# Layer 1's expert-weight products: five float32 values a node, or nine bf16 pairs on 96 partitions

## The chip, the cores and the metric

The kernel runs on one core of a Trainium2 chip, as one program. The metric is the device time of one execution in microseconds (us). The core's engines each work through a list of their own, in order: PE (matrix products; its weight loads are shown as PEld), DVE (vectors), ACT (activation functions and copies), POOL (here mostly the issue of gathers by index) and SP (the issue of plain transfers). Where one needs what another makes, it waits on a semaphore.

## The reference

A graph of 6250 nodes with 256 features and 106250 edges goes through two layers. Layer 0 is a two-step graph convolution, a linear attention and a feed-forward block with eight experts, one for each node. Layer 1 is a graph mean, a channel attention with an MLP, and a feed-forward block with four experts, two for each node, beside a shared MLP. The change concerns that last block:

```python
xn = _layernorm(x)
x = x + _L1_gnn_ref(xn, ...) + _L1_mix_ref(xn[None], ...)[0]
f = _layernorm(x)
# _L1_ffn_ref(f):
h = relu(einsum('baf,efh->ebah', f, eW1) + eb1)       # 4 experts, 256 -> 128
h = relu(einsum('ebah,ehg->ebag', h, eW2) + eb2)      # 128 -> 64
all_out = einsum('ebag,ego->ebao', h, eW3) + eb3      # 64 -> 256
shared = (three layers: sW1, sW2, sW3, with biases)   # 256 -> 256 -> 128 -> 256
topv, topi = top_k(softmax(f @ gW + gb), 2)
topw = softmax(topv)
out = shared + sum over the two chosen experts of topw * all_out
x = x + out
```

So every node has four expert weights (two of them zero) and the constant 1 for the shared bias: five numbers, called `we` below. The output must be float32 and agree with the reference.

## The kernel before

Nodes are held in 49 tiles of 128 rows (`NT`), edges in 831 chunks of 128 (`NCH`), sorted by destination, about 17 chunks to a node tile (`PER`). There are three passes over the edges. In each, POOL gathers the 128 source rows of a chunk by index (L542, one instruction a chunk, issued four at a time into one of three buffers in layer 1), DVE makes one-hot matrices for four chunks (L546), and PE multiplies the rows with the one-hots into running sums (L565). The first pass gathers float32 rows; the second and third gather rows that were split beforehand into three bf16 parts which add up to the float32 number exactly, so that a chunk is six short bf16 products.

Before the first pass, the edges are sorted into place, the rows are normalized, and a first table `t1f` is written by SP (L317) from DVE's and ACT's rows. The second pass also holds layer 0's expert block: `route` finds each node's expert and its slot, counts the nodes of each expert (`count`, L944) and sends the rows to their slots a planned 16 us later (`send`, by `later`); `pick` reads `count` to choose the next expert whose 128 rows are served.

The third pass is layer 1. Two jobs run beside its sums, each on a group of two node tiles, 25 groups in all:

- `mixing` (L1379 on): normalize, transpose (`xn3tr`, L263), attention product `att` (L1397), statistics, transpose (`hmtr`, L1412), fc1 with Gelu on ACT (L1420, L1422), fc2 on top of the self product `ws` (L1428, L1432).
- `feed` (L1451 on): the neighbour product (`neigh`, L1462), statistics, transpose (`f3tr`), the gate (L1482) and its softmax and top-two selection in about two dozen small DVE operations that end with `we` (L1509); the shared MLP (`s1`, `s2`) and the experts' first layer (`e1`, L1524, evacuated by DVE at L1526); then the part of the change: `we` is transposed to five rows `wet` (L1537, copied by ACT at L1538); the second expert layer for a pair of experts (L1545); `wexp` (L1550) spreads the weights over the pair's 128 hidden rows by a product with the selection matrix `sel`; DVE multiplies (L1551); and the output sums the shared product (L1558), the biases weighted by `wet` (`eb3`, L1559, with the shared bias `sb3` as the fifth row) and the two pairs (L1561). DVE adds the input and SP stores.

The order on PE, SP and POOL is written out by a planner, `pace` (L593 on): every `yield a, b` of a job says that the part just issued takes `a` us and that its result is there `b` us later; a chunk of sums is given 1.25 us in all, of which 0.23 us are its own. Between two chunks the planner issues those parts of the jobs that are due. When a job has nothing due, only chunks are issued. A feed starts when the sums of its two tiles are issued and its mixing is done; mixing starts at most six tiles ahead of the sums. What is left when the chunks are over is issued at the end (`rest`). The order on DVE and ACT is chosen by the compiler's scheduler. ACT loads a table whenever it goes from one of Sqrt, Exp and Gelu to another.

PSUM in layer 1 has four banks for products, used in turn (`mm`), one for transposes (`tr`), one for accumulation (`acc`) and two for sums. The constants `eb3`, `sel`, `wets` are made at the start of layer 1 (L1235 to L1238, L1265 to L1268, L1273 to L1277), partly by POOL ahead of its first gather there.

Of the kernel before, what the change touches and what calls it, by code (L numbers as in the profile page):

```python
# [31 lines left out]
F32 = mybir.dt.float32  # L32
BF16 = mybir.dt.bfloat16
I32 = mybir.dt.int32
AF = mybir.ActivationFunctionType
ALU = mybir.AluOpType
AX = mybir.AxisListType

P = 128
N = 6250  # L40
C = 256
# [63 lines left out]
NEXP = 8  # L105
# [33 lines left out]
def gps_kernel(ctx: ExitStack, tc: tile.TileContext, i: dict, out: bass.AP):  # L139
# [68 lines left out]
    rank8 = consts.tile([P, 8], F32, name="rank8")  # L208
    nc.vector.tensor_scalar(rank8, iota_f[:, :8], -1.0, 8.0, op0=ALU.mult, op1=ALU.add)

    deg = consts.tile([P, NT], F32, name="deg")
    dinv = consts.tile([P, NT], F32, name="dinv")
    rdeg = consts.tile([P, NT], F32, name="rdeg")
# [442 lines left out]
    nc.sync.dma_start(wout, i["L0_mix_W_out"])  # L656
    nc.sync.dma_start(boutr, row_bcast(i["L0_mix_b_out"], C))

    general_sums(t1, True)


# [235 lines left out]
    def route(v, t0, n):  # L897

        w = n * P
        f = work.tile([P, 2, C + 1], F32, name="f", bufs=3)  # L900
        for t in range(n):
            T = t0 + t
            normalize(f[:, t, :C], xa[:, T, :], mv1[:, T, :], rs1[:, T:T + 1])
        nc.vector.tensor_copy(f[:, :n, C:], mark[:, t0:t0 + n, None])
        yield 0.0, 4.0
        ft = work.tile([P, 2, 2 * P], F32, name="ft")
        transposed(ft, lambda t: f[:, t, :], n, "ftr", vs)
        yield 0.45 * n, 1.0
        for ht in hidden(ft, w):
            yield 0.43 * n, 0.0  # L910
        lt = ps_acc("gate")[:NEXP, :w]
        for m in range(8):
            nc.tensor.matmul(lt, lhsT=wg[:, m, :], rhs=ht[:, m, :w], start=(m == 0), stop=(m == 7))
            if m % 2 and m < 7:
                yield 0.43 * n, 0.0
        ls = work.tile([NEXP, 2 * P], F32, name="ls")
        nc.vector.tensor_scalar(ls[:, :w], lt, bgc, None, op0=ALU.add)
        yield 0.43 * n, 1.0
        tr = ps_tr("gate_t")
        for t in range(n):  # L920
# [12 lines left out]
        nc.vector.tensor_copy(ob, one)  # L933
        yield 0.3 * n, 6.0

        before = ps_acc("rank")[:, :n * NEXP]
        for t in range(n):
            b = before[:, t * NEXP:(t + 1) * NEXP]
            nc.tensor.matmul(b, lhsT=onesb, rhs=run[v], start=True, stop=False)
            nc.tensor.matmul(b, lhsT=upto, rhs=ob[:, t, :], start=False, stop=True)  # L940
            nc.vector.tensor_add(run[v], run[v], ob[:, t, :])
        cp = ps_tr("count")[:1, :NEXP]
        nc.tensor.matmul(cp, lhsT=onesb[:, 0:1], rhs=run[v], start=True, stop=True)
        nc.vector.tensor_copy(count[v], cp)  # L944
        at = small.tile([P, n, NEXP], F32, name="at")
        nc.vector.tensor_tensor(at, before.rearrange("p (t e) -> p t e", e=NEXP),
                                rb[v][:, None, :].to_broadcast([P, n, NEXP]), op=ALU.add)
        nc.vector.tensor_mul(at, at, one)
        to = small.tile([P, n], F32, name="slotf")
        nc.vector.tensor_reduce(to, at, AX.X, ALU.add)  # L950
        nc.vector.tensor_copy(slots[:, t0:t0 + n], to)
        yield 0.2 * n, 0.0

        def send():
            for t in range(n):
                r = rows_of(t0 + t)
                nc.gpsimd.indirect_dma_start(
                    out=xs[v][:, :], out_offset=bass.IndirectOffsetOnAxis(ap=slots[:r, t0 + t:t0 + t + 1], axis=0),
                    in_=f[:r, t, :], in_offset=None)
            routed[0] = t0 + n  # L960

        later(lag[0], send)
# [267 lines left out]
    for e in range(4):  # L1230
# [1 line left out]
        nc.sync.dma_start(ew1[:, :, e, :], i["L1_ffn_eW1"][e].rearrange("(k p) h -> p k h", p=P))  # L1232
        nc.sync.dma_start(ew2[:, e, half * 64:half * 64 + 64], i["L1_ffn_eW2"][e])
        nc.sync.dma_start(ew3[half * 64:half * 64 + 64, e // 2, :], i["L1_ffn_eW3"][e])
    eb3 = wl.tile([P, C], F32, name="eb3")  # L1235
    nc.gpsimd.memset(eb3, 0.0)
    nc.sync.dma_start(eb3[0:4, :], i["L1_ffn_eb3"])
    nc.sync.dma_start(eb3[4:5, :], i["L1_ffn_sb3"][None, :])  # L1238
    bfc1 = wl.tile([P, 6], F32, name="bfc1")
    nc.sync.dma_start(bfc1, columns(i["L1_mix_b_fc1"], 6))  # L1240
    ng = wl.tile([P, 2], F32, name="ng")
# [18 lines left out]
    nc.gpsimd.tensor_add(bsum, bsum, bf2r)  # L1260
    bxf = wl.tile([P, C], F32, name="bxf")


    seli = wl.tile([5, 2, 2, 64], I32, name="seli")
    nc.gpsimd.iota(seli, pattern=[[2, 2], [1, 2], [0, 64]], base=0, channel_multiplier=-1)  # L1265
    sel = wl.tile([P, 2, P], F32, name="sel")
    nc.gpsimd.memset(sel, 0.0)
    nc.vector.tensor_scalar(sel[:5], seli.rearrange("p a b c -> p a (b c)"), 0.0, None, op0=ALU.is_equal)  # L1268
    wstack = ExitStack()
    work = pool(wstack, "work3", bufs=1)  # L1270


    wets = []  # L1273
    for b in range(2):
        wet = wl.tile([P, 2 * P], F32, name=f"wet{b}")
        nc.gpsimd.memset(wet, 0.0)
        wets.append(wet)  # L1277

    xos = []
    for b in range(3):  # L1280
# [170 lines left out]
    def feed(t0, n):  # L1451
# [55 lines left out]
        nc.vector.tensor_tensor(o2, o2, d[:, :, None].to_broadcast(bc), op=ALU.mult)  # L1507
        nc.vector.tensor_add(o1, o1, o2)
        nc.vector.tensor_tensor(we[:, :, 0:4], o1, rd[:, :, None].to_broadcast(bc), op=ALU.mult)  # L1509
        yield 0.5 * n, 0.0  # L1510

        s1t = work.tile([P, 2, 2 * P], F32, name="s1t")
# [21 lines left out]
        wet = wets[t0 // 2 % 2]  # L1534
        tr = ps_tr("wet")
        for t in range(n):
            nc.tensor.transpose(tr[:5, t * P:(t + 1) * P], we[:, t, :], ident)  # L1537
        nc.scalar.copy(wet[:5, :w], tr[:5, :w])  # L1538
        yield 0.2 * n, 0.8

        e2t = work.tile([P, 2, 2 * P], F32, name="e2t")
        for pair in range(2):
            e_ps = ps_mm("e2_ps")
            for e in range(2):
                nc.tensor.matmul(e_ps[:, :w], lhsT=ew2[:, 2 * pair + e, :], rhs=e1t[:, 2 * pair + e, :w],  # L1545
                                 start=(e == 0), stop=(e == 1))
            nc.scalar.activation(e2t[:, pair, :w], e_ps[:, :w], AF.Relu, bias=eb2[:, pair:pair + 1], scale=1.0)
            yield 0.43 * n, 0.0
            w_ps = ps_mm("wexp")
            nc.tensor.matmul(w_ps[:, :w], lhsT=sel[:, pair, :], rhs=wet[:, :w], start=True, stop=True)  # L1550
            nc.vector.tensor_mul(e2t[:, pair, :w], e2t[:, pair, :w], w_ps[:, :w])  # L1551
            yield 0.22 * n, 0.0
        yield 0.0, 0.8

        for t in range(n):
# [4 lines left out]
            for pair in range(2):  # L1560
                nc.tensor.matmul(y, lhsT=e2t[:, pair, s], rhs=ew3[:, pair, :], start=False, stop=(pair == 1))  # L1561
            nc.vector.tensor_add(x3[:, t, :], x3[:, t, :], y)
            yield 1.72, 0.0
        if t0 + n < NT:
            nc.sync.dma_start(tiles_of(out, t0, n), x3[:, :n, :])
        else:
# [40 lines left out]
```

## Time and profile before

| | |
|---|---|
| median of 13 runs | 4452.33 us (4441.56 to 4474.08) |
| the profiled execution's own time | 4448.36 us |
| its span, first to last instruction | 4446.4 us |
| busy: PE / PE weight loads / DVE / ACT / POOL | 3309.8 / 2719.3 / 1417.8 / 949.7 / 2543.6 us |
| before the first pass's sums | 0 to about 98 us |
| layer 1, from its first instruction on POOL to the end | 3070.9 to 4446.4 us |
| wexp in layer 1 (L1550): PE records, busy | 100, 33.0 us |
| biases by weights (L1559): PE records, busy | 98, 30.2 us |
| transposes of `we` (L1537): PE records, busy | 49, 9.6 us |
| table loads on ACT in layer 1 | 79, 1283 ns each |

All times are from one profiled execution. The busy time of PE is the sum of durations of pipelined matmuls, which overlap; the distance between two starts says how long a matmul holds PE. A float32 product is two PE records, a bf16 product one. In the groups of instructions, out and in are tile names without buffer numbers; in the list of waits stand the total, how often, and the longest. In the timeline a row merges equal instructions in a row: start, length, count, and the idle time before it.

### The profile page before, as it was taken

What the parts mean: (1) busy time and instruction counts of PE and PEld (TensorE: products, weight loads), DVE (VectorE), ACT (ScalarE), POOL (GpSimd) and SP (SyncE); (2) the same over time, 40 slices, a digit from 0 to 9 for tenths busy, and PEclk for the clock granted to TensorE, in tenths of its full rate; (3) what the DMA queues carried; (4) which work ended last, traced back from release to release, by engine and by line L of the source; (5) the groups of instructions that cost most, each with busy time, mean ns of one, the idle gap of its engine ahead of it and who ended that gap; (6) DMA issues with size and microseconds to landing.
All of it is one profiled execution on the core that took longest, in us unless ns stands there. A gap on an engine that the chain in (4) does not pass through costs nothing. (4 is left out here: it accounts for less than half of the span.)

```text
span 4446.4 us, 60555 instructions
## 1 busy us (share of the span) xinstructions
PE 3309.8 (74%) x23423; PEld 2719.3 (61%) x23423; DVE 1417.8 (32%) x5275; ACT 949.7 (21%) x2019; POOL 2543.6 (57%) x2665
## 2 busy tenths in 40 slices
PE   3788776667655657877777788884788888888888
PEld 2577666666553446655555566663576676676676
DVE  6222222122221222222223322644433333443333
ACT  3111000000001112232222223441122222222222
POOL 1666666666656666666666565112666666666562
PEclk9888766666666678888888898997899999999999
DMA  4466433433344455555555665575444444444442
GB/s 154 132 169 167 119 114 116 116 116 116 115 127 135 125 147 158 172 174 172 172 164 160 202 188 158 178 238 156 124 133 127 133 129 128 131 129 134 130 129 68
DMA packets 341389, 639.63 MB, mean 144 GB/s; under 512 B 57498, under 2 KB 230341, under 8 KB 341088
## 3 DMA queue, kind: packets, MB, share of 16 engines
q0 software_dynamic: 151872, 450.67, 35.3%
q1 hardware_dynamic: 188366, 184.56, 13.5%
q8 instruction: 185, 3.03, 0.3%
q14 instruction: 116, 0.95, 0.1%
q10 hardware_dynamic: 850, 0.43, 0.0%
HBM read 559.64 MB, written 75.80 MB: 143 GB/s over the span
## 5 line engine op out<-in xcount | busy, mean ns | idle before, releaser
L542 POOL DMA_INDIRECT parts<-t3b,sp x831 | 807.4, 972 | 506.6 <-issue 199.1
L542 POOL DMA_INDIRECT parts<-t2b,sp x831 | 806.9, 971 | 486.6 <-issue 221.0
L542 POOL DMA_INDIRECT rows<-t1f,sp x831 | 804.1, 968 | 482.8 <-issue 225.3
L565 PEld LDWEIGHTS <-parts 128*128 128x128 bf16 x9972 | 600.5, 107 | 349.0 <-issue 138.4
L565 PE MATMUL sums<-onehotf,rows 128*128 128x84 f32 (+1 forms) x3324 | 595.8, 328 | 291.7 <-issue 224.3
L565 PEld LDWEIGHTS sums<-onehotf,rows 128*128 128x128 f32 x3324 | 579.9, 247 | 342.3 <-issue 311.2
L565 PE MATMUL sums<-onehot,parts 128*128 128x84 bf16 (+2 forms) x9972 | 687.1, 215 | 107.3 <-DMA parts<-t2b,sp 54.2
L892 PE MATMUL hid<-ft,fw 128*128 128x256 f32 (+1 forms) x1824 | 549.4, 441 | 45.6 <-ACT ht L894 28.1
L546 DVE TENSOR_TENSOR onehot<-iota_w,lof 128x336 bf16<-128x336 bf16 x416 | 210.2, 506 | 744.1 <-PE sums L565 314.8
L892 PEld LDWEIGHTS hid<-ft,fw 128*128 128x128 f32 x1824 | 370.1, 221 | 106.0 <-ACT ht L894 32.9
L894 ACT ACTIVATE ht<-hid,fb 128x256 f32<-128x256 f32 (+1 forms) x456 | 209.7, 472 | 437.6 <-PE hid L892 263.1
L546 DVE TENSOR_TENSOR onehotf<-iota_wf,lof 128x336 f32<-128x336 f32 x208 | 104.0, 507 | 623.3 <-remote 454.3
L1075 PE MATMUL exp<-wd,ht 128*128 128x256 f32 x1024 | 259.5, 391 | 5.6 <-ACT ht L894 5.6
L768 PE MATMUL h<-w,aggt 128*128 128x256 f32 x392 | 156.1, 538 | 107.6 <-DVE aggt L586 48.4
L585 ACT COPY aggt<-sums 128x88 f32<-128x88 f32 x96 | 22.4, 233 | 865.6 <-PE sums L565 538.6
L1075 PEld LDWEIGHTS exp<-wd,ht 128*128 128x128 f32 x1024 | 185.8, 192 | 30.4 <-ACT ht L894 8.5
L1047 POOL DMA_INDIRECT ys<-y,to x64 | 63.6, 994 | 220.9 <-DVE y L1080 76.1
L768 PEld LDWEIGHTS h<-w,aggt 128*128 128x128 f32 x392 | 93.2, 263 | 129.7 <-DVE aggt L586 51.8
L1420 PE MATMUL fc_ps<-ht,fc 128*128 128x256 f32 (+1 forms) x600 | 162.5, 394 | 1.7 <-issue 1.1
L1432 PE MATMUL fc_ps<-fc,ut 128*128 128x256 f32 x588 | 159.3, 395 | 3.7 <-issue 3.5
L1420 PEld LDWEIGHTS fc_ps<-ht,fc 128*128 128x128 f32 x600 | 106.8, 196 | 12.1 <-issue 1.1
L1432 PEld LDWEIGHTS fc_ps<-fc,ut 128*128 128x128 f32 x588 | 103.2, 191 | 14.2 <-issue 5.0
(354 smaller groups left out, 4274.2 us busy)
## 6 DMA issues: line engine op xcount, KB each, us to landing
wd<-in_L_ffn_Wd SPq DMA_DIRECT2D x64, 1024.0 KB
xs<-zero SPq DMA_DIRECT2D x8, 1799.0 KB
rows<-t1f,sp POOLq DMA_INDIRECT x831
parts<-t2b,sp POOLq DMA_INDIRECT x831
parts<-t3b,sp POOLq DMA_INDIRECT x831
t2b<-t2s SPq DMA_DIRECT2D x49, 192.0 KB
t3b<-t3s SPq DMA_DIRECT2D x24, 384.0 KB
fs<-xs SPq DMA_DIRECT2D x64, 128.5 KB
```

Of the source, the lines that this page charges most:

```text
L542: nc.gpsimd.indirect_dma_start(out=gs[:, j, :], out_offset=None, in_=(table if f32 else parts)[:, :], in_offset=bass.IndirectOffsetOnAxis( ...
L546: nc.vector.tensor_tensor(ohs[:, :n, :], (iota_wf if f32 else iota_w)[:, None, :WIN].to_broadcast([P, n, WIN]), lof[:, c:c + n, None].to_b ...
L565: nc.tensor.matmul(ps[b][:, h, n0 - b * P:n1 - b * P], lhsT=g[:, k * C + h * P:k * C + (h + 1) * P], rhs=oh[:, n0 - w0:n1 - w0], start=Fal ...
L585: nc.scalar.copy(dst[:, :, WIN:], sums[:, :, WIN:P])
L768: nc.tensor.matmul(h, lhsT=at[:, k, :], rhs=w[:, k, :], start=(k == 0), stop=(k == 1))
L892: nc.tensor.matmul(h_ps[:, :w], lhsT=fw1[:, k, m * P:(m + 1) * P], rhs=ft[:, k, :w], start=(k == 0), stop=(k == 1))
L894: nc.scalar.activation(ht[:, m, :w], h_ps[:, :w], AF.Gelu, bias=fb1[:, m:m + 1], scale=1.0)
L1047: nc.gpsimd.indirect_dma_start(out=ys[v][:, :], out_offset=bass.IndirectOffsetOnAxis(ap=to, axis=0), in_=y, in_offset=None)
L1075: nc.tensor.matmul(y_ps, lhsT=ht[:, m, q * P:(q + 1) * P], rhs=wd[:, m, :], start=(m == 0), stop=(m == 7))
L1420: nc.tensor.matmul(u_ps[:, :w], lhsT=fc1[:, k, m * P:(m + 1) * P], rhs=ht[:, k, :w], start=(k == 0), stop=(k == 1))
L1432: nc.tensor.matmul(h_ps, lhsT=ut[:, m, t * P:(t + 1) * P], rhs=fc2[:, m, :], start=False, stop=(m == 5))
```

## The change

`we` is split into three bf16 parts on DVE that add up to it exactly (`wes`, six copies with repetition and two subtractions for a group of two tiles). The 15 columns of a row are five values of part 0, then of part 1, then of part 2, and this row stands three times, at columns 0, 32 and 64 (the rest stays zero). The transpose becomes a product with a bf16 identity, which gives 96 rows. `sel` holds ones for all parts in all three places; `eb3` holds the three exact bf16 parts of the biases, part j in rows 32j and on, each repeated for the three parts of the weights. So one bf16 product sums all nine pairs of parts, where a float32 product stood. The constants move to the start of the program, with nine loads of the expert biases and three of the shared bias in place of one each; POOL's five fills at the start of layer 1 go. The planned times of the parts are made smaller. Apart from that, layer 0's `count` is set when the rows are sent, by way of a small copy, and not when they are counted.

```diff
+    identb = consts.tile([P, P], BF16, name="identb")
+    nc.vector.tensor_copy(identb, ident)
+    sel = consts.tile([P, 2, P], BF16, name="sel")
+    eb3 = consts.tile([P, C], BF16, name="eb3")
+    wets = [consts.tile([P, 2 * P], BF16, name=f"wet{b}") for b in range(2)]
+    wes = [consts.tile([P, 2, 3, 32], BF16, name=f"we{b}") for b in range(2)]
+    for b in range(2):
+        nc.vector.memset(wets[b], 0.0)
+        nc.vector.memset(wes[b], 0.0)
...
+        seli = early.tile([P, 2, 2, 64], I32, name="seli")
+        nc.gpsimd.iota(seli, pattern=[[2, 2], [1, 2], [0, 64]], base=0, channel_multiplier=-1)
+        self_ = early.tile([P, 2 * P], F32, name="self")
+        nc.vector.tensor_copy(self_, seli.rearrange("p a b c -> p (a b c)"))
...
+        nc.vector.tensor_scalar(acc, self_, 0.0, None, op0=ALU.is_equal)
+        for k in (-5.0, -10.0):
+            nc.vector.tensor_scalar(one, self_, k, None, op0=ALU.is_equal)
+            nc.vector.tensor_add(acc, acc, one)
+        nc.vector.tensor_copy(sel.rearrange("p a m -> p (a m)"), acc)
+        whole3 = early.tile([P, C], F32, name="eb3w")
+        nc.vector.memset(whole3, 0.0)
+        for j in range(3):
+            for k in range(3):
+                nc.sync.dma_start(whole3[32 * j + 5 * k:32 * j + 5 * k + 4, :], i["L1_ffn_eb3"])
+            nc.sync.dma_start(whole3[32 * j + 4:32 * j + 5, :], i["L1_ffn_sb3"][None, :])
+        part = early.tile([P, C], BF16, name="eb3p")
+        for j in range(3):
+            s = slice(32 * j, 32 * j + 32)
+            nc.vector.tensor_copy(part, whole3)
+            nc.vector.tensor_copy(eb3[s, :], part[s, :])
+            nc.vector.tensor_sub(whole3, whole3, part)
+        nc.vector.memset(eb3[96:, :], 0.0)
...
-        nc.vector.tensor_copy(count[v], cp)
+        soon = small.tile([1, NEXP], F32, name="counted", bufs=4)
+        nc.vector.tensor_copy(soon, cp)
...
+            nc.vector.tensor_copy(count[v], soon)
             routed[0] = t0 + n
...
-    eb3 = wl.tile([P, C], F32, name="eb3")
-    nc.gpsimd.memset(eb3, 0.0)
-    nc.sync.dma_start(eb3[0:4, :], i["L1_ffn_eb3"])
-    nc.sync.dma_start(eb3[4:5, :], i["L1_ffn_sb3"][None, :])
...
-    seli = wl.tile([5, 2, 2, 64], I32, name="seli")
-    nc.gpsimd.iota(seli, pattern=[[2, 2], [1, 2], [0, 64]], base=0, channel_multiplier=-1)
-    sel = wl.tile([P, 2, P], F32, name="sel")
-    nc.gpsimd.memset(sel, 0.0)
-    nc.vector.tensor_scalar(sel[:5], seli.rearrange("p a b c -> p a (b c)"), 0.0, None, op0=ALU.is_equal)
...
-        wet = wl.tile([P, 2 * P], F32, name=f"wet{b}")
-        nc.gpsimd.memset(wet, 0.0)
...
+        wb = wes[t0 // 2 % 2]
+        for k in range(3):
+            at3 = [wb[:, t, :, 5 * k:5 * k + 5] for t in range(n)]
+            for t in range(n):
+                nc.vector.tensor_copy(at3[t], we[:, t, None, :].to_broadcast([P, 3, 5]))
+            if k < 2:
+                nc.vector.tensor_sub(we, we, wb[:, :n, 0, 5 * k:5 * k + 5])
         yield 0.5 * n, 0.0
...
-            nc.tensor.transpose(tr[:5, t * P:(t + 1) * P], we[:, t, :], ident)
-        nc.scalar.copy(wet[:5, :w], tr[:5, :w])
-        yield 0.2 * n, 0.8
+            nc.tensor.matmul(tr[:96, t * P:(t + 1) * P], lhsT=wb[:, t].rearrange("p j r -> p (j r)"), rhs=identb,
+                             start=True, stop=True)
+        nc.scalar.copy(wet[:96, :w], tr[:96, :w])
+        yield 0.07 * n, 0.8
...
-            yield 0.22 * n, 0.0
+            yield 0.06 * n, 0.0
...
-            yield 1.72, 0.0
+            yield 1.4, 0.0
```

The lines of the two products themselves (L1550, L1559) stay as they are; their operands are now bf16. In the built program the lists of the first two passes keep their order on PE, and that of layer 1 on PE, DVE and ACT is another one.

More of the change, by code (lines that the diff above doesn't have):

```diff
@@ L657, in gps_kernel @@
     nc.sync.dma_start(boutr, row_bcast(i["L0_mix_b_out"], C))
+    with ExitStack() as st:
+        early = pool(st, "early")
+        seli = early.tile([P, 2, 2, 64], I32, name="seli")
+        nc.gpsimd.iota(seli, pattern=[[2, 2], [1, 2], [0, 64]], base=0, channel_multiplier=-1)
+        self_ = early.tile([P, 2 * P], F32, name="self")
+        nc.vector.tensor_copy(self_, seli.rearrange("p a b c -> p (a b c)"))
+        one = early.tile([P, 2 * P], F32, name="selone")
+        acc = early.tile([P, 2 * P], F32, name="selacc")
+        nc.vector.tensor_scalar(acc, self_, 0.0, None, op0=ALU.is_equal)
[16 more added lines that the diff above has]
+        nc.vector.memset(eb3[96:, :], 0.0)
     general_sums(t1, True)
@@ L1261, in gps_kernel @@
     bxf = wl.tile([P, C], F32, name="bxf")
-    seli = wl.tile([5, 2, 2, 64], I32, name="seli")
-    nc.gpsimd.iota(seli, pattern=[[2, 2], [1, 2], [0, 64]], base=0, channel_multiplier=-1)
-    sel = wl.tile([P, 2, P], F32, name="sel")
-    nc.gpsimd.memset(sel, 0.0)
-    nc.vector.tensor_scalar(sel[:5], seli.rearrange("p a b c -> p a (b c)"), 0.0, None, op0=ALU.is_equal)
     wstack = ExitStack()
     work = pool(wstack, "work3", bufs=1)
-    wets = []
-    for b in range(2):
-        wet = wl.tile([P, 2 * P], F32, name=f"wet{b}")
-        nc.gpsimd.memset(wet, 0.0)
-        wets.append(wet)
     xos = []
```

## The prediction

> **What bounds the kernel now.** I read the page's busy rows and slices first, then the busy time by stage.
>
> ```profile
> PE 3309.8 (74%) x23423; PEld 2719.3 (61%) x23423; DVE 1417.8 (32%) x5275; ACT 949.7 (21%) x2019; POOL 2543.6 (57%) x2665
> PE   3788776667655657877777788884788888888888
> POOL 1666666666656666666666565112666666666562
> 3200.00:4390.00 1190.00, 1012.71 (x7998) 828.18 (x7997) 472.07 (x1655) 272.32 (x574) 726.95 (x749) 0.93 0.46 130
> 4390.00:4446.40 56.40, 40.95 (x226) 34.76 (x223) 21.03 (x89) 16.94 (x35) 0.00 (x0) 0.90 0.03 11
> ```
>
> The columns of the last two lines are stretch, length, then busy time of PE, PEld, DVE, ACT, POOL, then clock. All edited products lie after 3200 us, in layer 1. There PE is busy 85% at a granted clock of 0.93, POOL 61%, DVE 40%, ACT 23%. Who is waited for there, in the list of waits of PE from 3070 us on (total us, times, longest):
>
> ```profile
> PE xn3tr L263 <- DVE xnt L267: 43.8, 18, 5.2
> PE f3tr L263 <- DVE ft L267: 38.3, 25, 5.5
> PE hmtr L1412 <- DVE ht L1413: 16.1, 18, 2.9
> PE sums L565 <- DMA parts<-t3b,sp: 11.9, 1, 11.9
> PE ffn L1558 <- DVE x L1562: 10.3, 9, 3.1
> PE wet L1537 <- DVE we L1509: 2.9, 1, 2.9
> ```
>
> The gathers starve PE once; the rest are chains through DVE and ACT before a transpose. L1486 (once a group) starts at 3214.9 and, 22 groups on, at 4355.5: 51.8 us a group, of some 34 chunks, while POOL could issue 34 gathers in 34 x 1.25 = 42.5 us (below). So PE's in-order stream sets the pace: its own work, plus waits in front of three transposes, none of them in the edited lines.
>
> **What one edited product costs.** Timelines of PE and POOL, and the chain of waits near the end:
>
> ```profile
> 3997.37 1.10 PE L1524 MATMUL e_ps<-ft,ew 128*128 128x256 f32 x4
> 3998.31 0.39 PE L565 MATMUL sums<-onehot,parts 128*128 128x84 bf16 x6
> 3998.53 1.10 PE L1524 MATMUL e_ps<-ft,ew 128*128 128x256 f32 x4
> 3581.78 0.34 PE L558 MATMUL sums<-zrow 128*128 128x424 bf16 x1
> 3581.96 0.39 PE L565 MATMUL sums<-onehot,parts 128*128 128x84 bf16 x6
> 4412.40 0.22 PE wet L1537 x2
> 4415.22 0.43 PE wexp L1550 x2
> 4419.10 0.43 PE ffn L1559 x2
> 3564.67 0.94 POOL L542 DMA_INDIRECT parts<-t3b,sp  x1 [0.30 <-issue]
> ```
>
> Durations overlap, so prices are distances between starts. A float32 product is two records: 0.43 us on the chain (0.94 for two in the timeline). A bf16 matmul of 424 columns holds PE 3581.96-3581.78 = 0.18 us, so 256 columns take 0.108; six of 84 columns, with six weight loads, take 0.22, which gives 0.112. The built program has each edited product as one load and one matmul.
>
> - wexp (L1550): 48 x (0.43-0.108) + 2 half-wide x 0.16 = 15.8 us off PE.
> - eb3 (L1559): 49 x 0.322 = 15.8 us off.
> - wet (L1537): 49 x (0.11-0.055) = 2.7 us off.
>
> Together **-34.3 us** of PE time, before anything replaces it. Bounds: -38 by the 0.94 row, 0 if every saving turns into waiting (rival 2).
>
> **What is added.**
>
> - *DVE splits* (six copies, two subtractions a group, 197 in all). Nearest row: L1509, 128x8, 168 ns; bounds 60 ns (memset L1506) and 411 ns (copy L267), so 12 to 81 us of DVE work, 33 at 168 ns, 1.35 us a group. They sit behind L1509 and ahead of two e1t evacuations (L1526), whose PSUM banks come round again four tiles later, and ahead of one-hots that are three buffers deep. In the group at 3580 us L1509 started at 3588.59 and wet at 3593.92: 5 us of cover. If it were gone, wet would wait. The last group has no cover: five operations, 0.85 us. I take **+2**, range 0 to +33.
> - *ACT order.* In the built program layer 1 has 79 table loads before and 100 after. From about the fifteenth group on, Gelu is cut by Exp twice and Sqrt once. Cause: the smaller yields (each feed is planned 1.5 us shorter) let feed catch up with the gathers, after which it waits for its next sums tile and drifts against mixing. Before, one group has that pattern, the last two-tile one:
>
> ```profile
> 4405.42 1.28 ACT L1422
> 4407.10 1.28 ACT L1501
> 4409.52 1.13 PE L1524 MATMUL e_ps<-ft,ew 128*128 128x256 f32 x4 [0.25 <-DVE e1t L1526]
> ```
>
> Both loads are on the chain, yet PE idled only 0.25 us after them, since other products were queued. So 21 x 1.283 = 27 us if all show, some 3 if all are covered like this. Behind a load wait Gelu, s1t and the d that DVE needs for wet; s1t's banks are needed four products on. Nearer the covered end, I take a quarter, **+7**.
>
> The Trainium skill (ScalarE: Activation LUTs, What ACT_TABLE_LOAD costs) speaks against this change: it gives 1283 ns for the load and some 1380 ns more for a drain. By that page 21 switches would be an estimated 56 us and the change a loss. This trace has the 1.28 but not the drain: the Gelu after the load at 4405.42 started at 4406.71.
>
> - *The drift itself.* After the drift the order puts three to five chunks of sums before the transposes hmtr and f3tr; four chunks are 4 x 0.22 = 0.9 us of PE, while att to hmtr needs 0.41+0.42+0.17+0.30+0.16+0.78 = 2.2 us through L1399, L223, L224, L228, L229, L232. But xn3tr no longer comes right behind neigh's statistics, and mixing's and feed's chains run side by side, so the 43.8 and 38.3 us of waits above may shrink. Unsigned: **0**, from -40 to +48 (rivals 1 and 3).
> - *Early block.* Twelve loads at 0.43 us on SP: six stand before the first t1f store (they wait for a memset behind DVE's work that ends at 70.5; the store went at 74.11), five in the gap up to 78.35, one after the last store. Eight DVE operations (0.31 to 0.42 each) fill DVE's idle 2.83 us before 73.32; the nine of the split wait for the loads but stand behind the first one-hots, with 8 us idle before 105.95. If that cover were gone: 12 x 0.43 = 5. **+0.5**, range 0 to +5. POOL's early iota lies far ahead of its first gather (98.4).
> - *Count repair.* 25 copies of 1x8 on DVE, 0.17 us at most each, in a stage where DVE is under a third busy; the same number of chunks is served, perhaps in another order of experts: **0**, range 0 to +4.
> - ACT's copy of wet goes from 5 to 96 partitions with the same 256 columns (354 ns): 0.
>
> **What is moved.** Five POOL fills leave the start of layer 1, where the chain of waits passes through POOL's first gather:
>
> ```profile
> 3071.33 0.31 POOL L1236 MEMSET eb<- 128x256 f32 x1
> 3072.87 1.00 POOL L542 DMA_INDIRECT parts<-t3b,sp  x1 [0.17 <-issue]
> ```
>
> **-1.5 us**; bounds 0 (if DVE's one-hot at 3073.37 holds PE) and -1.5. The two SP loads removed there are not waited for. The tail: after the last sums (4395.6) the old order still has a mixing and two feeds, the new one the end of a feed and one more. PE work is only shifted, but of the old tail's 45 us about 10 are waits (from 4390 on 56.4 less 41 busy, less the 5.8 after PE's end at 4440.6); I take **-3**, from 0 to -10. The chain through neigh, f3tr, gate and wet of the last tile stays.
>
> **Sum:** -34.3 +2 +7 +0 +0.5 +0 -1.5 -3 = -29. The profiled execution took 4448.36 us (span 4446.4), 4 under the median 4452.33; it would become 4419, and the median **4423**.
>
> **Rivals.**
>
> 1. *Slower:* in the last ten groups the table loads and the uncovered att chain land on PE. For it: both loads on the chain at 4405; against: PE idled 0.25 us there. Price: two loads and the 2.2 us chain are 4.8 us a group, 48 in ten; in place of the +7 this gives -36+48 = +12: 4464. It decides from 3.6 us a group.
> 2. *No change:* PE reaches the three transposes earlier and waits the difference. For it: those waits total 98 us and DVE sets their ends. Against: L1550 and L1559 stand eight or more products before them, and DVE is 60% idle. Price: 4450.
> 3. *Much faster:* the new phase removes waits, and groups approach POOL's 42.5 us. Ten groups, 4 us each of the 9 between: -40 more, 4383; all nine 4333.
>
> That the products are not cheaper is excluded by the bf16 rows.
>
> **Numbers.** 0.2% is 9 us, about what a measurement of this kernel can tell from no change. Forecast (4395 to 4443) 0.60; rival 1 0.14; rival 2 0.12; rival 3 0.14. Faster 0.60+0.14 = 0.74, same 0.12, slower 0.14. The range leaves out about a tenth on each side: 4380, inside rival 3, to 4462, inside rival 1.
>
> **What would show it.** Wexp and ffn L1559 at one record each, some 0.11 us apart; 50 and 49 rows for 100 and 98; PE busy after 3200 us down by some 35; the first gather of layer 1 1.5 us earlier after L1228; 100 table loads in layer 1, their cost seen as PE waits for ut (L1422 in the old numbering) and hmtr in the last 400 us. Wrong if the early groups, with their order nearly unchanged, do not shrink from 52 to about 50.5 us, or if the last ten grow past 54.

## The result, and the profile after

The change made the kernel slower where a gain of 29 us had been forecast: a median of 4484.34 us (4476.75 to 4509.75, 11 runs) against 4457.35 us for the kernel before (48 runs), ratio 1.0074 with a 95% interval of 1.0059 to 1.0090. The profiled execution of the changed kernel took 4458.62 us (span 4456.8), 26 us under its median, where that of the kernel before lay 9 us under its own; two profiles alone would have shown 10 us for a loss of 27 by the medians and 33 by the ratio.

Page rows of the changed kernel, and its busy time by stage (stretch, length, then PE, PEld, DVE, ACT, POOL, PE's granted clock, DMA share, GB/s):

```profile
PE 3301.7 (74%) x23324; PEld 2702.2 (61%) x23324; DVE 1459.7 (33%) x5519; ACT 976.7 (22%) x2040; POOL 2544.7 (57%) x2661
PE   3788766767655667787777878784788888888877
3200.00:4390.00 1190.00, 987.73 (x7764) 801.41 (x7763) 499.89 (x1832) 298.18 (x590) 710.09 (x732) 0.90 0.45 127
4390.00:4456.80 66.80, 46.08 (x353) 37.26 (x350) 25.14 (x107) 17.87 (x39) 16.82 (x18) 0.93 0.22 65
```

In the same 1190 us PE is busy 25 us less than before, and less is done (732 instructions on POOL, not 749). The granted clock is 0.90, not 0.93; the prediction had read that figure and then left it alone.

The three edited products and the table loads on ACT (two views of the changed kernel: instructions by line with duration min/median/max, then groups with total and mean):

```profile
L1585 PE MATMUL wexp<-wet,sel x50: 216/272/417, 3234.2 to 4448.0; 128*128 128x256 bf16 x48, 128*128 128x128 bf16 x2
L1594 PE MATMUL ffn<-eb,wet x49: 269/273/421, 3240.3 to 4449.1; 128*128 128x256 bf16 x49
L1541 DVE CAST we<-we 128x15 bf16<-128x15 f32 x147 | 19.7, 182 | 2.1
L1543 DVE TENSOR_TENSOR we<-we,we 128x10 f32<-128x10 f32 (+1 forms) x50 | 8.5, 170 | 1.3
L1448 ACT ACT_TABLE_LOAD x38 | 48.8, 1283 | 50.3 <-PE fc_ps L1446 35.9 <-issue 8.4 <-PE sums L577 3.8
```

(The durations of products overlap with their neighbours'.) One record each, 50 and 49 for 100 and 98. From start to start wexp and the bias product hold PE for 0.109 us and the product that makes `wet` for 0.061: the unit prices were right. The splits take 28 us of DVE, 33 had been reckoned.

PE's waits in layer 1 after the change (us in total, times, longest):

```profile
PE f3tr L275 <- DVE ft L279: 43.4, 21, 5.4
PE xn3tr L275 <- DVE xnt L279: 40.7, 20, 5.9
PE hmtr L1438 <- DVE ht L1439: 26.5, 20, 4.4
PE hmtr L1438 <- DVE xm L244: 17.5, 4, 8.7
PE ffn L1593 <- DVE x L1597: 16.0, 9, 3.0
```

One more row of the kernel before belongs beside them:

```profile
PE hmtr L1412 <- DVE xm L232: 4.8, 2, 3.9
```

Against the list of before, hmtr has gained 23 us (26.5 + 17.5 for 16.1 + 4.8), `ffn` 6; the waits put down to ACT add up to 9.3 us for 5.7, although its table loads went from 79 to 100. From its first gather to the end layer 1 took 1391.0 us, 1373.5 before (profiles of the second and third group gave 1384.5 before and 1391.9 and 1395.2 after). So in this pair 17.5 us were lost where the prediction's terms for this stage add up to a gain of 30. Where these 47 us went took experiments.

### The profile page after: what moved, and what is told of

Its sections match the earlier page's. It is cut to its first block, busy times and chain, and to the rows that moved or that the text cites. A ratio compares the mean times of both kernels' runs of the same rounds, so it can differ in the third digit from the quotient of the medians.

```text
span 4456.8 us, 60586 instructions
## 1 busy us (share of the span) xinstructions
PE 3301.7 (74%) x23324; PEld 2702.2 (61%) x23324; DVE 1459.7 (33%) x5519; ACT 976.7 (22%) x2040; POOL 2544.7 (57%) x2661
## 5 line engine op out<-in xcount | busy, mean ns | idle before, releaser
L1446 PE MATMUL fc_ps<-ht,fc 128*128 128x256 f32 (+1 forms) x600 | 171.6, 412 | 4.5 <-DVE e1t L1560 3.4
```

The costliest lines, as they stand in the source:

```text
L1446: nc.tensor.matmul(u_ps[:, :w], lhsT=fc1[:, k, m * P:(m + 1) * P], rhs=ht[:, k, :w], start=(k == 0), stop=(k == 1))
```

## The experiments

The kernels that stand together below ran on one chip, and the chips were of two kinds. Where the result was measured, and for the second and third group, the kernel before takes 4457 to 4459 us, for the first, fourth and fifth group 3968 to 3975 us. Chips of these two kinds are called A and B below (the theories A to F in the expectations are another matter); the profile that the prediction read is from an A. Ratios are to the kernel before on the same chip, with 95% intervals, and us are worked out from them.

### First group (a B chip): order, products, splits and count apart

Old planned times in the changed kernel:

```diff
-        yield 0.07 * n, 0.8
+        yield 0.2 * n, 0.8
-            yield 0.06 * n, 0.0
+            yield 0.22 * n, 0.0
-            yield 1.4, 0.0
+            yield 1.72, 0.0
```

> The changed kernel with the three planned times of the old one (0.2, 0.22 and 1.72 a tile); the order on PE in layer 1 is then that of the kernel before (23 feeds that start at the same chunks, 79 table loads), with the cheap products, the splits, the early constants and the count repair kept. Theory A (the smaller planned times cost the loss: feed catches up with the gathers, and the table loads and longer chains land on PE): the products' -34 us show, less some splits, so a ratio of 0.992 to 0.996 to the kernel before. Theory B (the products' form itself costs: the splits on DVE, or a lower granted clock under bf16 products, eat the saving): ratio 1.004 to 1.010, like the changed kernel, and the clock in the first half of layer 1 near 0.90 in place of 0.93. Theory C (the loss comes from ahead of layer 1, the early constants or the count repair): also 1.004 to 1.010, but with layer 1 itself shorter by some 30 us.

Measured 0.9909 (0.9891 to 0.9928), -36 us: what the products were reckoned to bring (-34), and a little more.

The opposite edit in the kernel before (new planned times, float32 products):

> The kernel before with nothing changed but the three planned times (0.07, 0.06 and 1.4 a tile): the new order, 100 table loads in layer 1, with the float32 products. Theory A: the order alone costs what the products' -34 us and the measured +33 us add up to, some 67 us: ratio 1.012 to 1.018. Theory B: the order costs little: 0.998 to 1.003. Theory C: the same, 0.998 to 1.003.

Measured 1.0010 (0.9996 to 1.0024): +4 us. Theory A in its first form, an order that costs 67 us, falls on this chip.

The count repair alone:

```diff
-        nc.vector.tensor_copy(count[v], cp)
+        soon = small.tile([1, NEXP], F32, name="counted", bufs=4)
+        nc.vector.tensor_copy(soon, cp)
...
+            nc.vector.tensor_copy(count[v], soon)
             routed[0] = t0 + n
```

> The kernel before with nothing changed but the count repair (layer 0's counts are set when the rows are sent). Theories A and B: 0.999 to 1.001. Theory C in the form of the count repair: some part of +33 to +67 us, 1.007 to 1.015, to be seen as a longer second stage (it was 1754 us before and 1747 us after in the profiled executions).

Measured 0.9996 (0.9979 to 1.0012): nothing. Its profile serves below as that of the kernel before on a B chip, with the same order on PE.

Old planned times, first part of the weights only:

```diff
-        for k in range(3):
+        for k in range(1):
...
-            if k < 2:
-                nc.vector.tensor_sub(we, we, wb[:, :n, 0, 5 * k:5 * k + 5])
```

> As the kernel with the old planned times and the cheap products, but of the weights only the first bf16 part is made (two copies a group in place of six and two subtractions; the second and third parts are left zero, so the weights are rounded). The difference to that kernel is the price of 147 DVE operations. Theory A: the splits have cover: 0 to 5 us faster than the kernel with all parts. Theory B in the form of the splits: 15 to 33 us faster than it. Theory C: no difference.

Measured 0.9893 (0.9874 to 0.9912), 6 us under the kernel with all parts and within the two intervals. So on this chip none of the parts, tried alone, is slow, which no theory had foreseen. What was missing was the changed kernel itself, on this kind of chip.

### Second group (an A chip)

> The changed kernel once more, unchanged. In the runs so far the kernel before took 3975 us, not 4457: they came from a chip on which every pass over the edges is shorter (pass 1 1071 us for 1198). There the old planned times with the cheap products gave 0.991 and the new ones with the dear products 1.001. Theory D (the order and the products add up, and the loss belongs to the slow chip alone): 0.990 to 0.994 on a chip with about 3975 us, and again 1.006 to 1.009 if the kernel before takes about 4450. Theory E (cheap products and new order together make something that neither makes alone, such as a feed that runs against the chunks in the last ten groups): 1.004 to 1.010 on either.

> The changed kernel with the three old planned times, unchanged from its first run, beside the changed kernel on one chip. Theory D: 0.989 to 0.993 on a fast chip, within 4 us or so of the changed kernel; on a slow one (about 4450 us) also near 0.992, so that there the order alone costs 65 us. Theory E: 0.989 to 0.993 on either, 55 to 75 us under the changed kernel on either.

> The kernel before, for its profile on the chip of these runs: 0.998 to 1.002 by every theory. Layer 1, from its first gather to the end, should take 1195 to 1205 us on a fast chip (it was 1373.5 in the first profile), with PE's waits of 4 us and more gone.

The changed kernel gave 1.0048 (1.0028 to 1.0069), +21 us; the old planned times 0.9974 (0.9953 to 0.9996), -12 us. The kernel before took 4456.71 us once, layer 1 of it 1384.5 us. So the loss was repeated, and the same edit that brought 36 us on a B chip brought 12 here. Theories D and E had both put the old planned times at 0.989 to 0.993 on such a chip, and both missed.

What differs between the chips can be read from one program. Busy time and clock, then the kernel before's two transposes' copies on DVE (total, mean ns | idle before, and what ended it), on A (the profile of the prediction) and on B (with the count repair):

```profile
3260.00:4380.00 1120.00, 953.45 (x7532) 779.83 (x7530) 443.80 (x1562) 256.00 (x541) 686.12 (x707) 0.93 0.46 130
L267 DVE COPY xnt<-xn3tr 128x256 f32<-128x256 f32 (+1 forms) x25 | 10.3, 411 | 20.3 <-remote 17.9 <-PE xn3tr L263 2.3
L267 DVE COPY ft<-f3tr 128x256 f32<-128x256 f32 (+1 forms) x25 | 10.3, 411 | 6.4 <-remote 5.4 <-PE f3tr L263 0.7
```

```profile
2950.00:3880.00 930.00, 868.56 (x7218) 720.58 (x7217) 428.82 (x1505) 246.16 (x514) 662.37 (x679) 0.97 0.54 151
L267 DVE COPY ft<-f3tr 128x256 f32<-128x256 f32 (+1 forms) x25 | 10.2, 409 | 0.6 <-PE f3tr L263 0.5
L267 DVE COPY xnt<-xn3tr 128x256 f32<-128x256 f32 (+1 forms) x25 | 10.2, 407 | 1.0 <-PE xn3tr L263 1.0
```

The copies themselves take 0.41 us on both, and so does everything on DVE, ACT and POOL that I compared (one-hots 506 and 504 ns, Gelu 474 and 474, a gather 971 and 976). But on A DVE sits idle before the copy for "remote", that is for nothing the profile sees. One such case on A, PE's timeline, DVE's timeline, and the stretches around it:

```profile
3358.90 0.56 PE L263 MATMUL f3tr<-ident,f 128*128 128x128 f32 x2
3364.95 0.69 PE L263 MATMUL f3tr<-ident,f 128*128 128x128 f32 x2 [5.50 <-DVE ft L267]
3364.47 0.42 DVE L267 COPY ft<-f3tr 128x256 f32<-128x256 f32 x1 [2.51 <-remote]
3359.40:3363.70 4.30, 0.05 (x1) 0.00 (x0) 1.26 (x4) 0.00 (x0) 2.83 (x3) 1.00 0.57 151
3363.70:3370.60 6.90, 5.65 (x33) 5.04 (x34) 2.77 (x11) 1.04 (x4) 1.86 (x2) 0.51 0.14 37
```

PE's second transpose waits 5.5 us for DVE's copy of the first; DVE does the copy at 3364.47 and had nothing else to do from 3361.96 on; the copy's input had gone into PE at 3358.90. The trace of semaphores tells the same: the one that the copy waits for is raised by PE alone, four PE instructions whose records end by 3359.5 raise it, and its updates came at 3361.52, 3364.38, 3364.41 and 3364.45. So the wait that the list calls "PE f3tr <- DVE ft" was PE's own result, late by up to 5 us, and right behind it the clock record falls to one half for 6.8 us. On B the longest wait of that name is 2.6 us.

The clock record knows two values, 1 and 0.5, in steps of 3.4 us. In the profile of before, there are 33 falls to one half between the first and the last gather of layer 1: in the 3.4 us ahead of a fall PE was busy 26% on average, in the 286 steps after which the clock stayed full 91% (at least 46%). So on A a half-clock phase follows, on average, a step in which PE mostly stood.

The list of before had 43.8 and 38.3 us for xn3tr and f3tr; on B, with the same order:

```profile
PE f3tr L263 <- DVE ft L267: 28.0, 25, 2.6
PE xn3tr L263 <- DVE xnt L267: 18.1, 25, 1.2
PE hmtr L1414 <- DVE ht L1415: 16.9, 24, 1.3
```

To see how much of A's extra time belongs to such places, I laid PE's records of layer 1 (from 150 us after its first gather) of an A and a B profile with the same order beside each other, one by one, and added up by how much each step from start to start was longer on A. "Share in half clock" is the part of that excess in steps that touch a half-clock stretch, and beside it the share of the time that such steps make up:

| kernel (A against B) | products | order | excess, us | of it PE idle | share in half clock | of the time |
|---|---|---|---|---|---|---|
| before, two profiles | float32 | old | 155, 161 | 106, 110 | 56%, 60% | 17%, 18% |
| new planned times alone | float32 | new | 156 | 102 | 67% | 21% |
| before, without the bias products | float32 | old | 158 | 105 | 63% | 20% |
| old planned times | bf16 | old | 186 to 193 | 120 | 62% | 21% |
| changed kernel, three profiles | bf16 | new | 194, 193, 198 | 127, 130, 122 | 59%, 69%, 67% | 23% to 26% |

(Partners on B: the count repair, the new planned times alone, the old planned times in four profiles, two of them with five busy rows, and for the changed kernel the one with five busy rows and all splits of the fourth group. Against the changed kernel's own profile of the fifth group the last row would be 184 to 189. The steps across the missing bias products are left out.) Three things follow. A's extra time is bunched at the half-clock phases, about three times as dense there as over the whole stretch. Two thirds of it is PE standing idle, one third longer steps while it is busy. And with bf16 products there is some 25 to 40 us more of it, in either order, while neither the order alone nor leaving out the float32 bias products alters it. Half-clock time in the same stretch, up to the last gather, is 154 and 162 us before, 166 without the bias products, 184 with cheap products, 199 with the new order, 221, 215 and 236 with both; on B 58 before, 34 to 48 with cheap products, 61 with the new order, 51 to 72 with both. PE's waits of over 2 us in that stretch, added up, grow only with both: 84 and 94 us before, 81 without the bias products, 82 with cheap products, 95 with the new order, 122, 123 and 115 with both; on B they are 3 to 8 us.

### Third group (an A chip)

> The changed kernel, a third time. So far: on a chip where the kernel before takes 3975 us the old order with cheap products gave 0.9909 and the new order with dear ones 1.001; where it takes 4458 us the old order with cheap products gave 0.9974 and the changed kernel 1.0048. On the slower chip the granted clock goes to one half in phases of 3.4 or 6.8 us for 147 us of the last 1125 us of gathers (before) and 212 of 1157 us (changed kernel); on the other for some 50. Theory F (the throttle: on the slower chip saved PE time is partly given back, and the new order costs more there): 0.990 to 0.996 on a fast chip, 1.004 to 1.009 on a slow one. Theory E (products and order together make it slow): 1.004 or more on either.

> The kernel before with the three new planned times alone. Theory F: on a slow chip the order costs as it does between the two kernels with cheap products, some 33 us: 1.005 to 1.010; on a fast one again 1.000 to 1.003. Theory E: 0.998 to 1.003 on either.

The time planned for a chunk at 1.20 us:

```diff
-  (lambda: ahead and ahead[0] <= now[0] / 1.25 / PER + 6, mixings, 1)], 1.25, factor=1.0)
+  (lambda: ahead and ahead[0] <= now[0] / 1.20 / PER + 6, mixings, 1)], 1.20, factor=1.0)
```

> The changed kernel with the time planned for a chunk of layer 1 at 1.20 us for 1.25: a feed then comes every 33 chunks to the end, none catches up, and there are 79 table loads, with the smaller planned times kept. If the catching up (and not the planned times themselves) is what costs: like the kernel with the old planned times, 0.989 to 0.993 on a fast chip, 0.995 to 0.999 on a slow one, and perhaps a few us less. If the costs of the order lie elsewhere: like the changed kernel.

The kernel before without the bias products:

```diff
-            nc.tensor.matmul(y, lhsT=wet[:, s], rhs=eb3, start=False, stop=False)
```

> The kernel before without the 49 float32 products of the biases (the output leaves out the experts' and the shared bias): 49 x 0.43 = 21 us of PE work gone, with no bf16 product, no split and no order changed. Theory F: on a slow chip only a third or so comes off, -5 to -10 us (0.9978 to 0.9989), on a fast one the whole, -18 to -24 us (0.994 to 0.9955). If instead the bf16 products draw the throttle by their own form, the whole -18 to -24 us comes off on either chip.

The changed kernel gave 1.0038 (1.0018 to 1.0059), the new planned times with float32 products 1.0011 (0.9993 to 1.0030), a feed every 33 chunks 1.0011 (0.9996 to 1.0027), and the kernel without bias products 0.9961 (0.9939 to 0.9983). In us: +17, +5, +5, -17.

The second expectation of theory F missed: the order alone is cheap on A too. So on A the bf16 products brought nothing in the new order and by the medians made it worse by some 12 us (+17 against +5, with intervals that overlap), where on B they bring 36 in the old one. The slot kernel missed as well (+5, not -4 to -22), and its profile says where: its gathers take 1315.4 us like those of the old planned times on A (1313.3), and not 1344 to 1349 as in the new order, but from the last gather to the end it needs 72.7 us for 60.7, since feeds that come later leave more behind. Taking away 21 us of float32 work gave 17 (interval 8 to 27): work that is only removed comes off on A, more or less whole, and the excess of A over B stays at 158 us without it. So theory F, by which A gives back two thirds of any saving (5 to 10 us left), is not supported; the interval only touches its range.

### Fourth group (a B chip)

What was open: whether the throttle (the half-clock phases) answers to the 45 busy rows of the new products, or the splits on DVE cost, on A. Two edits, each with old and new planned times: the first part alone (as in the first group), and all splits made but only five rows copied:

```diff
-        nc.scalar.copy(wet[:96, :w], tr[:96, :w])
+        nc.scalar.copy(wet[:5, :w], tr[:5, :w])
```

> Old planned times, cheap products, only the first bf16 part of the weights (no subtractions, two copies a group; the output uses rounded weights). Where the kernel before takes 4458 us, old planned times with all parts gave 0.9974. Theory S (the splits on DVE cost where PE runs slower and DVE's queue is later): 10 to 20 us less, 0.993 to 0.9955. Theory H (products with 45 busy rows of 96 draw the throttle that five rows did not): also less, 0.993 to 0.9955, with fewer half-clock phases in layer 1 (about 150 us after its first 190, for 179). Neither: 0.996 to 0.999. On a fast chip 0.9893 again.

> The same with the new planned times. The changed kernel gave 1.0038 to 1.0074, the new times with dear products 1.0011. Theories S and H: 0.999 to 1.002. Neither: 1.003 to 1.007. On a fast chip the changed kernel has not been timed: some 0.990 to 0.996 if order and products add up.

> Old planned times, cheap products, all splits made on DVE, but only five rows of the transposed weights are copied (the output uses the first part of the weights and of the biases alone), so that the products have five busy rows as before the change. Theory S: as with all rows, 0.9965 to 0.9985. Theory H: 10 to 20 us less, 0.993 to 0.9955, with the half-clock time of layer 1 back at about 150 us. Neither: 0.996 to 0.999.

> The same with the new planned times. Theory S: 1.003 to 1.007, like the changed kernel. Theory H: 0.999 to 1.002. Neither: 1.003 to 1.007.

Measured 0.9912 (0.9889 to 0.9934), 0.9930 (0.9908 to 0.9953), 0.9899 (0.9877 to 0.9921) and 0.9965 (0.9950 to 0.9979). The chip was a B, so the question about A stayed unanswered, and no later run takes it up. What the four do tell: with the old order neither the splits nor the rows cost anything on B (0.9893 to 0.9912 whatever is left out). With the new order all cheap-product kernels are 7 to 26 us slower than with the old one; the difference between the two new-order kernels, 14 us for the splits, has intervals that just overlap.

### Fifth group (a B chip)

> The changed kernel, beside the next two on one chip. The slower chips (4458 us for the kernel before) gave 1.0038 to 1.0074, and on the faster ones (3971 to 3975 us) it was not timed. There the new order cost 4 to 27 us and the cheap products brought 36, so 0.992 to 0.997 if the chip is a fast one (theory F, the throttle; 'products and order together' would give 1.004). On a slow one 1.003 to 1.008.

> Old planned times with the cheap products and all rows: 0.989 to 0.993 on a fast chip, 0.995 to 1.000 on a slow one (0.9974 there before).

> The same with five busy rows (the output uses the first part of the weights and biases alone; all splits are made). On a fast chip 0.988 to 0.992, as with all rows. On a slow one: theory H (the throttle answers to the 45 busy rows) 0.989 to 0.993, 15 to 25 us less than with all rows; if it answers to anything else, such as the shorter time between the other products, within 8 us of the kernel with all rows.

The changed kernel: 0.9955 (0.9935 to 0.9975), -18 us. Old planned times 0.9908 (0.9891 to 0.9924), -37; with five rows 0.9911 (0.9892 to 0.9930). So on a B chip the change is a gain, as theory F had it (theory E wanted 1.004 on either chip), and the new order takes half of what the products bring.

Where the order costs, in the last 550 us of layer 1 on B, changed kernel first, then old planned times:

```profile
PE hmtr L1438 <- DVE xm L244: 10.0, 7, 2.8
PE hmtr L1438 <- DVE ht L1439: 8.1, 12, 1.1
PE f3tr L275 <- DVE ft L279: 7.7, 13, 0.9
PE xn3tr L275 <- DVE xnt L279: 6.1, 11, 0.8
PE wet L1571 <- DVE we L1541: 5.2, 2, 4.0
```

```profile
PE f3tr L275 <- DVE ft L279: 12.0, 13, 1.7
PE xn3tr L275 <- DVE xnt L279: 8.1, 12, 1.2
PE hmtr L1438 <- DVE ht L1439: 7.0, 10, 1.2
PE f3tr L275 <- DVE f L244: 6.4, 9, 2.3
PE wet L1571 <- DVE we L1541: 4.0, 1, 4.0
```

A new row leads: hmtr waits 10 us for `xm`, seven times, which is the chain from `att` through DVE and ACT that the prediction had called uncovered. f3tr and xn3tr give back some 6 us. The same row for `xm` stands at 9.9 us with float32 products in the new order and at 10.0 without the splits: it belongs to the order, and it does not say why the order costs more with bf16 products. Waits on ACT are 1.2 us in the whole layer, as they are before the change on B. One place in the timelines of PE, ACT and DVE of the changed kernel on B:

```profile
3591.52 0.85 PE L577 MATMUL sums<-onehot,parts 128*128 128x84 bf16 x18
3593.13 0.56 PE L1438 MATMUL hmtr<-ident,xm 128*128 128x128 f32 x2 [0.76 <-DVE xm L244]
3589.15 1.28 ACT L240 ACT_TABLE_LOAD   x1
3590.45 0.29 ACT L240 ACTIVATE sd<-mvm,eps_t 128x2 f32<-128x2 f32 x1
3592.13 0.15 DVE L241 RECIPROCAL rsm<-sd 128x2 f32<-128x2 f32 x1
3592.59 0.72 DVE L244 TENSOR_SCALAR xm<-xm,mvm,rsm 128x256 f32<-128x256 f32 x2
```

Three chunks of sums in a row, and still 0.76 us of waiting behind them. The table load ended at 3590.43, 0.15 us after the statistics that `sd` reads (mvm, over at 3590.28), so it held `sd` for 0.15 us. `sd` is there at 3590.74, and DVE comes to its reciprocal only at 3592.13: neigh's evacuation and statistics (L1489, L235, L236) stand before it in DVE's order. So at this place the price of the drift is mainly a queue on DVE, not a table.

Start-to-start times of the gates, us a group, tell first half (12 groups, ahead of the drift) from second (9 groups, after the drift):

| | A, first | A, second | B, first | B, second |
|---|---|---|---|---|
| float32, old order | 52.1, 51.9 | 51.5, 52.2 | 44.9 | 45.0 |
| float32, new order | 50.1 | 56.8 | 44.8 | 47.9 |
| bf16, old order | 51.7 | 51.6 | 43.4, 42.9 | 43.0, 43.0 |
| bf16, new order | 51.3, 50.6, 51.1 | 55.5, 56.3, 55.6 | 42.9 | 47.4 |
| the same without splits; with five rows | | | 42.8; 43.1 | 46.9; 46.0 |

In the new order a group of the first half holds some 31 chunks, not 33, and one of the second some 34. The drift costs some 3 to 5 us a group on either chip, and feeds that have caught up shorten the end: from the last gather to the end 40 to 44 us for 59 to 61 on B. The two together, first gather to end on B, from the old order to the new, one profile each: 1197.6 to 1209.9 us with float32, 1155.4 to 1186.9 with bf16 (1163.5 to 1170.3 without the splits, 1154.3 to 1171.9 with five rows).

## Why the prediction was right or wrong

It was wrong on the chip it was made for, in sign; on the other kind its figure of -29 stands against -18 (-26 to -10). Step by step:

- **Price of a product, -34.3 us of PE.** The price is right: 0.109 and 0.061 us a product, and -36 and -37 us in the two timings of the old order on B with nothing left out. The first step that failed is the next one, "PE's in-order stream sets the pace: its own work, plus waits", with the clock of 0.93 taken as given: by it a saving of PE time is a saving of time. On A that same kernel brought 12 us (2 to 21), and its excess over B is some 30 us larger than that of the kernel before, 10 to 14 us of it as idle time of PE and the rest as longer steps, bunched at half-clock phases. The -12 lies inside the bounds of -38 to 0 that the term had, but with a part, the clock, that no rival named.
- **The reading of the waits.** "the rest are chains through DVE and ACT before a transpose": of the 82 us for xn3tr and f3tr some 36 are missing in the same list on B (46 us), and where A's trace was followed they were PE's own late results. The longest figures told it: 5.2 and 5.5 us in front of a copy that takes 0.41.
- **DVE splits, +2, range 0 to +33.** Right in the old order (0 within the intervals on B). In the new one they may cost 14 us on B; that is not settled, and on A their cost was not measured.
- **ACT order, +7.** 100 loads came as foreseen; PE's waits on ACT rose by 4 us on A (5.7 to 9.3) and not on B (1.2 us with and without the change). The Trainium skill (ScalarE: Activation LUTs, What ACT_TABLE_LOAD costs) would have added a drain to each; no run here shows one.
- **The drift, 0, and the tail, -3.** This is the second step that failed. Both terms were too small, with opposite signs: on B with bf16 the gathers take 26 to 48 us more and the end 16 to 20 less. The sum of the three order terms was reckoned at +4; with float32 it measured +4 and +5, with bf16 +7 to +26 on B and +33 on the A of the second group. That the sum came out with float32 products is luck, since its parts did not. Why the order costs more with bf16 products is open.
- **Early block, +0.5, range 0 to +5.** The first gather starts at 101.2 us (14 profiles, 100.5 to 101.9) for 97.7 (six, 96.7 to 99.3): +3.5, inside the range, in its upper half.
- **Count repair, 0.** Right: 0.9996.
- **POOL fills, -1.5.** Not to be seen: from the last gather of the second pass to the first of the third 302 to 310 us on A, with and without them, a spread that hides 1.5.
- **The rivals.** Rival 1 had the place (the last ten groups) and one of its two causes, the chain from `att` to hmtr, held up by DVE's queue; a group of the second half costs 3 to 5 us more where it said 4.8. Its table loads were not seen to matter, and the order alone would not have made the kernel slower on A. Rival 3, a phase without waits, had no support in any run. Of the signs named for being wrong, the late one was plain on A, last groups at 55.5 to 56.3 us; the early one is not clear, early groups at 51.3, 50.6 and 51.1 us instead of 50.5, and since they hold fewer chunks (50.1 us with float32 products too) they do not measure the products.

On A, by size: the changed kernel's -18 us on B, and 26 to 31 us more excess of A over B than the kernel before has (by its own profile on B), which gives +8 to +13 beside the measured +17 to +33; the excess was counted in a part of layer 1 alone. This is bookkeeping of runs and profiles, not a cause. That the additional time lies at half-clock phases and in long waits of PE is measured. That removed PE work brings these about was one reading, and the one run that tries it alone speaks against it: without the float32 bias products 17 of 21 us came off and the excess did not grow. What remains are the form of the bf16 products and the splits on DVE, and on A neither was tried alone, so the cause stays open.

The Trainium skill (TensorE: Matmul & The Clock Gate, Part 1) has a rule that fits the clock record and was not weighed: PE's clock is halved after at least one idle window of about 3.4 us and comes back after a busy one. The record here agrees in the step of 3.4 us and in what precedes a fall, with PE busy 26% and not idle throughout. But the falls alone do not account for the loss: there are 33 and 31 of them before, 37 with cheap products, 34 with the new order, 37 to 41 with both, and 38 without the bias products, where time was won. Why A chips have late results and B chips hardly any, no run here shows.

The version to keep is the one with the old planned times: 0.9974 (0.9953 to 0.9996) on an A and 0.9908 and 0.9909 on a B; it beats both kernels on both kinds.

## What to carry to other kernels

Before a saving on PE is booked, look at the granted clock of the stage and at the longest waits in front of DVE copies that are short themselves: where DVE idles for "remote" and the clock falls to one half right after, the wait can be PE's own late result, which a list of waits puts down to DVE, and a shorter instruction elsewhere need not shorten it (36 us came off on B, 12 on A). Change products and planned times in separate steps: here the planner's smaller times cost half of what the products brought on B. And a result from one chip is a result for that chip; the same two kernels stood at 1.005 on one and 0.9955 on another.

## What the runs showed that was not expected

- Chips that differ by 11%: 4458 and 3971 us for one program, with single instructions on DVE, ACT and POOL alike to 1%. The first pass takes 1198 and 1067 us, the second 1453 and 1274, layer 1 1374 and 1198 (the prediction's profile and that of the count repair); the stretch without gathers between the second and third pass is nearly alike, 308 and 299.
- Results of PE that reach DVE up to 5 us late, with next to no PE record in between, followed by a half-clock phase.
- An order that costs 4 us with float32 products and 19 to 33 with bf16 ones (changed kernel against old planned times, on B and on the A of the second group).
